# A depthwise 5x5 convolution moved from eight to sixteen tiles of the TensorE array, with its results kept by row phase

## The chip, the cores and the metric

The kernel runs on one core of a Trainium2 chip. The metric is the device time of one execution in microseconds. A core has a matrix engine (TensorE, PE in the profile; its weight loads are listed as PEld), a vector engine (VectorE, DVE), a scalar engine (ScalarE, ACT), GpSimd (POOL) and a queue that issues most DMAs (SyncE, SP). TensorE reads its operands from SBUF and writes to PSUM banks; the other engines copy results out of PSUM.

## The reference

The input x is (4, 128, 128, 128): four batches, 128 channels, 128 x 128 pixels, float32. The first layer is overlapping window attention and a gated feed-forward part with a depthwise convolution, the second a quantised pair of 3x3 convolutions:

```
# 9 x 9 overlapping regions of 16 x 16 pixels, step 14, 4 heads of 32
y = layernorm(tokens);  q, k, v = split(y @ w_qkv)
tok = softmax(q k^T / sqrt(32)) v @ w_out + b_out + tok
xf = overlap-average of tok            # (4, 128*128, 128)
y = layernorm(xf) @ w_p0 + b_p0        # 256 channels
ym = depthwise_conv5x5(y, dw_k, padding 2)
ym = batchnorm(ym over batch and pixels)
y = gelu(gelu(ym)) @ w_p2 + b_p2 + xf  # 128 channels
# second layer, x = y
q1 = round(15 clip(x, 0, 1)) ;  c1 = conv3x3(q1, quantised w1) ; batchnorm
q2 = round(15 clip(., 0, 1)) ;  c2 = conv3x3(q2, quantised w2) ; batchnorm
out = c2 + x
```

The batchnorm over all batches means that the gelu stage can start only when the depthwise convolution of all four batches is done, and likewise for the two later normalisations.

## The kernel before, in words

**Attention.** A band is one row of nine regions (j = 0 to 8); there are 36 bands, t = 0 to 35, nine for each batch. For region j of band t the order is written out by hand: `scores(j)` (L784; four heads side by side in four row tiles, into four PSUM banks held by two tiles `sc0` and `sc1`, one buffer each; ACT takes the exponentials, L792), then `values(j-1)` of the region before (L847, L855, into the bank `po`; DVE takes the reciprocal, L867, and two products), then four slots of side work that `beside(t)` plans: the layernorm and projections of band t+1 or t+2 (a1, a2), the output projection, second layernorm and 256-channel projection of band t-1 (b1, b2), and steps of the convolution (`c[j]`). `halves(j)` between the slots adds the two halves of the exponentials (POOL and DVE, L802). Every engine of the four named in MANUAL runs its instructions in this order; SP issues its DMAs in order too. `store` puts a DMA on a list, and `flush` issues after each step what was on the list before it.

**Layernorm by DMA.** The reciprocal deviations go to a row in DRAM (ACT's queue, L397) and come back spread over all partitions (`xn<-row`, L411, on SP).

**The depthwise convolution.** The projection's result y is stored to DRAM (`y_d<-y`, L431) as `y2_d`: rows, two column parities, 256 channels, 64 columns of one parity. Each channel is convolved as a banded matrix product: the contraction runs over 20 input rows x 2 parities (KD = 40 partitions), the output over 16 rows x 2 parities (32), and the columns are 8 row groups x 64 columns of a parity (512). Three shifts of one column make up the five columns of the kernel, accumulated in PSUM. Two halves of the partitions (row tiles of 64) and four column tiles hold eight channels at once: 24 matmuls for a tile of eight channels (`depthwise`, L601). A float32 matmul is two instructions in the profile. The result goes to two of the three `pm` banks, ACT copies both to SBUF (L648), DVE takes their statistics (L652), and they are stored to `cv_d` in rows of 64 floats (256 bytes). `conv_steps` gives 32 tiles for a whole batch (u loads for two tiles ahead, L634, weights, L587). Batches 0 to 2 are convolved beside the bands that start two after their last one: batches 0 and 1 over nine bands each (t = 10 to 27), batch 2 over five (28 to 32); of batch 3 four row groups over two bands, two over the last band, and the last two groups in `conv_rest` after attention, when the banks of the scores are free (L690, L721, L725, L730; weights by POOL's queue).

**Band matrices.** In the first ten bands a set of steps builds the banded weights in DRAM (`band_matrices`: `pad_d`, `band_d`, `dw_d`; 24 DVE copies at L268).

**Late stages.** `gelu_stage` reads `cv_d` in units of 8 rows (1024 pixels), applies batchnorm and two gelus on ACT (L1216, L1219), multiplies by w_p2 (L1228), adds xf on DVE (L1236; the convolution left each row as two parities, which this operation interleaves with a stride of two), stores the result to `id_d`, quantises it into `q1` (a padded fp8 image in SBUF), and runs the first 3x3 convolution (L1164, 18 matmuls a unit) two units behind. `last_stages` runs the second 3x3 convolution once for its statistics, three units behind the normalisation, keeps batch 3's result, and computes the others again in the last stage, where each unit is normalised, `id_d` is added and the output is stored (L1354).

## Time and profile before

| | us |
|---|---|
| median of 3 runs (lowest, highest) | 3247.21 (3236.61, 3251.82) |
| profiled execution | 3249.98 |
| its span | 3248.2 |

| stage of the profiled execution | from, to (us) |
|---|---|
| bands 0 to 9, no convolution | 27.1, 504.5 |
| bands 10 to 27, batches 0 and 1 convolved | 504.5, 1538.5 |
| bands 28 to 32, batch 2 convolved | 1538.5, 1911.9 |
| bands 33 to 35, batch 3 in part | 1911.9, 2193.6 |
| rest of batch 3's convolution | 2193.6, 2318.7 |
| gelu stage and first 3x3 convolution | 2318.7, 2798.2 |
| second 3x3 convolution | 2798.2, 3048 |
| last stage | 3048, 3248 |

A busy time is the time in which an engine had at least one instruction in flight; matmuls overlap, so a group's busy time divided by its count is far below the mean of one. The number behind the last bar of a group is the idle time just before its instructions, and what ended it. In the timeline, the first number is the start from the span's begin, the second the length of the merged stretch.

### The profile page before, as it was taken

Reading aid. Unit: us, or ns where it says so; the run is one execution under the profiler, and the core shown is the slowest. Engines: PE = TensorE matmul, PEld = TensorE weight load, DVE = VectorE, ACT = ScalarE, POOL = GpSimd, SP = SyncE. Lnnn points to the kernel's source line nnn. Section 1 sums busy time; section 2 is a strip of 40 time slices with the busy share of each in tenths; the row PEclk is TensorE's granted clock in tenths of the full one; section 3 lists DMA queues with packets and bytes.
Section 4 is the critical chain, followed back from the end, with each engine's and each line's share of the span. In section 5 each row is a group of like instructions: output and inputs, shape, how many; then the busy total and the mean of one; then the engine's idle time right before and its main releaser. Section 6 shows DMA issues by size and latency. Waiting matters only on the chain.

```text
span 3248.2 us, 92154 instructions
## 1 busy us (share of the span) xinstructions
PE 3059.6 (94%) x39162; PEld 1480.1 (46%) x39162; DVE 2014.5 (62%) x3244; ACT 1988.5 (61%) x2658; POOL 840.9 (26%) x1058
## 2 busy tenths in 40 slices
PE   7999999999999999999888998876899999999998
PEld 4555544444444444444344444453544444444443
DVE  5777886766766777676555664542455555666543
ACT  5777777777776777677555655432477777433443
POOL 3444443333333333333222232211111111000000
PEclk9999999999999999999999998876799999999999
DMA  3555677888886888886898988857899999452398
GB/s 82 151 167 162 176 186 191 203 199 204 215 193 169 191 206 211 196 213 172 179 202 201 209 188 203 196 158 187 264 354 359 358 359 304 162 167 80 110 357 311
DMA packets 809891, 681.70 MB, mean 210 GB/s; under 512 B 580918, under 2 KB 695935, under 8 KB 809471
## 3 DMA queue, kind: packets, MB, share of 16 engines
q1 hardware_dynamic: 798879, 669.17, 75.8%
q8 instruction: 311, 5.10, 0.7%
q0 software_dynamic: 1024, 3.93, 0.5%
q10 hardware_dynamic: 9568, 2.61, 0.3%
q14 instruction: 109, 0.89, 0.1%
HBM read 408.72 MB, written 270.79 MB: 209 GB/s over the span
## 4 chain that ended last, share of the span: by engine, by line
PE 76%; DMA 9%; ACT 5%; issue 4%; SPq 3%; DVE 2%; ACTq 0%; POOL 0%; DVEq 0%; POOLq 0%
PE pc L1164 21%; PE pm L438 16%; PE sc L784 9%; PE pm L601 9%; PE po L847 8%; PE pb L1228 6%; PE po L855 3%; DMA y_d<-y 3%; PE pm L377 3%; ACT pt L792 2%; DMA u<-y_d 2%; DMA xn<-row 1%; SPq L451 1%; SPq L431 1%; ACT v L775 1%
## 5 line engine op out<-in xcount | busy, mean ns | idle before, releaser
L867 DVE RECIPROCAL rd<-po 128x256 f32<-128x256 f32 x324 | 568.8, 1756 | 439.1 <-PE po L855 438.5
L1164 PE MATMUL pc<-q,wq 128*128 128x512 fp8e4 x3168 | 700.3, 381 | 5.1 <-DVE q L1176 5.1
L792 ACT ACTIVATE pt<-sc 128x1024 f32<-128x1024 f32 x648 | 628.2, 1025 | 119.1 <-PE sc L784 63.2
L802 POOL TENSOR_TENSOR sm<-pt 128x512 f32<-128x512 f32 x324 | 415.7, 1283 | 1047.3 <-ACT pt L792 727.0
L1164 PEld LDWEIGHTS <-wq 128*128 128x128 fp8e4 x3168 | 309.0, 98 | 406.7 <-issue 38.9
L784 PE MATMUL sc<-q,kr 32*128 32x256 f32 x5184 | 413.6, 417 | 27.3 <-ACT pt L792 27.1
L601 PE MATMUL pm<-u,w 40*32 40x504 f32 (+5 forms) x7680 | 369.6, 503 | 41.7 <-DMA u<-y_d 29.7
L784 PEld LDWEIGHTS sc<-q,kr 32*128 32x128 f32 x5184 | 254.1, 191 | 286.4 <-issue 177.1
L847 PE MATMUL po<-pt,v 128*32 128x256 f32 x5184 | 364.9, 401 | 10.0 <-DVE part L871 6.9
L648 ACT COPY c<-pm 128x512 f32<-128x512 f32 (+1 forms) x256 | 132.4, 563 | 272.3 <-PE pm L601 243.3
L438 PE MATMUL pm<-xn,wp 128*32 128x512 f32 (+1 forms) x2304 | 248.1, 553 | 44.6 <-ACT y L567 42.6
L567 ACT ACTIVATE y<-pm,vectors 128x512 f32<-128x512 f32 (+1 forms) x288 | 183.1, 641 | 166.0 <-DMA y_d<-y 111.9
L802 DVE TENSOR_TENSOR sm<-pt 128x512 f32<-128x512 f32 x324 | 244.2, 754 | 35.8 <-ACT pt L792 35.8
L438 PE MATMUL pm<-xn,wqkv 128*32 128x512 f32 (+1 forms) x2304 | 245.3, 548 | 4.9 <-ACT v L775 3.5
L601 PEld LDWEIGHTS pm<-u,w 40*32 40x32 f32 x7680 | 147.6, 112 | 223.1 <-issue 153.0
L652 DVE BATCH_NORM_STATS2 st<-c 128x6 f32<-128x512 f32 (+2 forms) x320 | 160.9, 550 | 134.8 <-ACT c L648 134.3
L1228 PE MATMUL pb<-cv,wp 128*128 128x512 f32 x512 | 232.1, 596 | 4.9 <-ACT cv L1219 4.9
L847 PEld LDWEIGHTS po<-pt,v 128*32 128x32 f32 x5184 | 140.5, 112 | 186.5 <-issue 103.5
L1172 DVE BATCH_NORM_STATS2 st<-pc 128x6 f32<-128x512 f32 x256 | 165.7, 689 | 84.7 <-PE pc L1164 84.7
L855 PE MATMUL po<-sm,ones 128*32 128x256 f32 x2592 | 206.1, 389 | 0.0
L874 POOL TENSOR_TENSOR ob<-ob,part 128x32 f32<-128x32 f32 x288 | 127.2, 442 | 230.6 <-DVE part L871 224.8
L438 PE MATMUL pm<-wqkv,yr 128*32 128x128 f32 x5184 | 176.3, 273 | 1.2 <-issue 1.2
(157 smaller groups left out, 3394.2 us busy)
## 6 DMA issues: line engine op xcount, KB each, us to landing
cv<-cv_d SPq DMA_DIRECT2D x64, 1024.0 KB
u<-y_d SPq DMA_DIRECT2D x234, 256.0 KB
cv_d<-c SPq DMA_DIRECT2D x192, 256.0 KB
y_d<-y SPq DMA_DIRECT2D x160, 256.0 KB
xn<-row SPq DMA_DIRECT2D x76, 512.0 KB
xfl<-xf_d SPq DMA_DIRECT2D x64, 512.0 KB
id_d<-y SPq DMA_DIRECT2D x64, 512.0 KB
idt<-id_d SPq DMA_DIRECT2D x64, 512.0 KB
```

The costliest lines, as they stand in the source:

```text
L438: nc.tensor.matmul(out[m], w[:, m], v, start=True, stop=True)
L567: nc.scalar.activation(y[:, :n], pm[:, : n * P].rearrange("p (r c e) -> p r e c", r=n, e=2), AF.Identity, bias=bp0[:, h : h + 1],)
L601: nc.tensor.matmul(outs[half][32 * q : 32 * q + 32, j, :, a:z], wt[hs, s, c, :], ut[hs, :, c, a + s - 1 : z + s - 1], start=(s == 1), stop ...
L784: nc.tensor.matmul(sc[h // 2][:, h % 2, kc, :].rearrange("p (r c) -> p r c", c=RS), region(kr, j)[hs, kc * P : (kc + 1) * P], queries(j, h ...
L792: nc.scalar.activation(pt, sc[p], AF.Exp)
L802: add(sm, pt[:, :, 0, :], pt[:, :, 1, :], ALU.add)
L847: nc.tensor.matmul(po[hs, 0, :], v[:, kc, hs], pt[h // 2][:, h % 2, kc, :], start=(kc == 0), stop=(kc == 1),)
L855: nc.tensor.matmul(po[hs, 1, :], ones, sm[h // 2][:, h % 2, :], start=True, stop=True)
L867: nc.vector.reciprocal(rd, po[:, 1, :])
L1164: nc.tensor.matmul(pc[:, h], w[:, t, :], q1[b][:, r + dy : r + dy + RB, dx : dx + P], start=(t == 0), stop=(t == 8),)
L1172: nc.vector.bn_stats(st[:, 2 * n + h, :], pc[:, h])
L1228: nc.tensor.matmul(pb[:, m], wp2[:, h, :], cv[:, h, px], start=(h == 0), stop=(h == 1))
```

## The change

The convolution is cut into sixteen tiles of 32 x 32. Output groups have 8 rows (GR = 8, sixteen groups), and the columns come in four phases (NC = 4), so that an output tile is 8 rows x 4 phases = 32; the contraction is 12 rows x 2 parities = 24 partitions (KD). Each of the four row tiles takes 64 of the 256 channels (channel 64 i + c is on partitions 32 i to 32 i + 23), the four column tiles take four channels; a step has sixteen channels. The input is still kept by two parities (IW = 64), so a matmul reads every second element; the five columns of the kernel and the four phases together need four shifts, so a step has 64 matmuls. The sixteen steps of a batch replace 32 tiles.

- A step writes to four banks, the two tiles of the score banks (`ps_s`), where a tile wrote to two of the three `pm` banks. ACT copies two banks out, DVE two (L687); statistics on DVE as before.
- Slots: even regions have the step first in the third slot, ahead of projections, odd ones last in the second. One or two steps a band take regions 4 and 8, then 2, 6, 0, and the odd ones last.
- Loads: a step of a whole batch reads two u tiles (three buffers in all) in sixteen DMAs and its weights in one. They are issued one step ahead, by a list `later` that runs after the next region's scores.
- `y2_d` is kept by row phase and parity, with channel and row group inside; a chunk of rows that crosses a group is stored in two DMAs. Input rows of a whole batch are read in runs of 4 KB. `cv_d` is kept so that a store writes 1 KB runs (half a batch) and a load of the gelu stage reads 4 KB.
- `conv_rest` has eight steps of 32 channels, which use the score banks and the `pm` and `po` banks in turn; its weights come in one DMA.
- The late stages go by row phase: a unit is 8 rows of one phase (every eighth row) of one half of the image, `xf_d` and `id_d` follow that order, the padded image `q1` holds phase by phase, the first 3x3 convolution runs three units behind and the second four. The second projection's sum on DVE now interleaves four phases (a stride of four elements), and an output unit is stored as eight rows of 512 bytes per channel.

```diff
-GR = 16
-CW = P // 2
+GR = 8
+NG = P // GR
+NC = 4
+CW = P // NC
+IW = P // 2
 KD = 2 * (GR + 4)
+NS = 16
...
-    y2_d = [dram.tile([P + 4, 2, 2 * P, CW], F32, name=f"y2_d{b}") for b in range(B)]
-    cv_d = [dram.tile([P // GR, 2 * P, GR * P], F32, name=f"cv_d{b}") for b in range(B)]
+    y2_d = [dram.tile([2 * GR, 2 * P, NG + 1, IW], F32, name=f"y2_d{b}") for b in range(B)]
+    cv_d = [dram.tile([2, 2 * P, 32, NG // 2, CW], F32, name=f"cv_d{b}") for b in range(B)]
...
+        def depthwise(outs, wt, ut):
+            for s, (a, z) in ((1, (0, CW)), (0, (1, CW)), (3, (0, CW - 1)), (2, (0, CW))):
+                for i in range(4):
+                    hs = slice(32 * i, 32 * i + KD)
+                    for q in range(4):
+                        nc.tensor.matmul(
+                            outs[i][32 * q : 32 * q + 32, :, a:z],
+                            wt[hs, s, q, :], ut(q)[hs, :, 2 * a + s - 1 : 2 * z + s - 2 : 2],
+                            start=(s == 1), stop=(s == 2),
+                        )
+        def fetch_input(ut, b, g, ch, below):
+            n, ng = ut.shape[1:3]
+            m = 8 if below else 2 * GR
+            for i in range(4):
+                at = 32 * i + 2 * GR * below
+                c = 64 * i + ch
+                nc.sync.dma_start(
+                    out=ut[at : at + m].rearrange("p c g x -> p c (g x)"),
+                    in_=y2_d[b][:m, c : c + n, g + below : g + below + ng].rearrange("p c g x -> p c (g x)"),
+                )
...
             def products(at):
-                k, jj, c0 = tiles[at]
-                ut, wt = U.pop(at), W[k, jj]
-                pc = [ps_m.tile([P, nj, ng, CW], F32, name="pm") for _ in range(2)]
-                depthwise(pc, wt[:, :, c0:], ut, nc_)
-                for half in range(2):
-                    cv = cp.tile([P, nj, ng, CW], F32, name=f"c{half}")
-                    nc.scalar.copy(
...
+                sc = [ps_s.tile([P, 2, 2, NT], F32, name=f"sc{p}") for p in range(2)]
+                banks = [
+                    sc[i // 2][:, i % 2].rearrange("p a n -> p (a n)")[:, : nk * w] for i in range(4)
+                ]
...
+                for i in range(4):
+                    cv = cp.tile([P, 2 * NT], F32, name="c")[:, : nk * w]
+                    (nc.vector.tensor_copy if i // 2 else nc.scalar.copy)(cv, banks[i])
+                    for m in range(nk):
+                        k = nk * at + m
+                        cm = cv[:, m * w : (m + 1) * w]
+                        nc.vector.bn_stats(stat(i, k, n), cm)
+                        gh = -(-ng // 8)
+                        store(results(b, g0, ng, i, k), cm.rearrange("p (h n) -> p h n", h=gh))
...
                 def one(at=at):
-                    if at + ahead < len(tiles):
-                        load(at + ahead)
+                    if at not in U:
+                        load(at)
                     products(at)
+                    if at + ahead < NS // nk:
+                        later.append(lambda: load(at + ahead) if at + ahead not in U else None)
...
-            for j in sorted((1, 3, 5, 7, 8, 4, 6, 2, 0)[: len(conv)]):
+            for j in sorted((4, 8, 2, 6, 0, 1, 5, 3, 7)[: len(conv)]):
...
-                ([a2[1]], [a1[4]], b1[:2], [*c[2], a2[2]]),
+                ([a2[1]], [a1[4]], [*c[2], *b1[:2]], [a2[2]]),
                 ([], [a2[3], *c[3]], [], [b1[2]]),
-                ([b1[3]], [a2[4]], [*a1[5:], *b2[:2]], [*c[4], b1[4]]),
+                ([b1[3]], [a2[4]], [*c[4], *a1[5:], *b2[:2]], [b1[4]]),
...
-                ([], [b2[6], x2], b1[7:], [*c[8], s1]),
+                ([], [b2[6], x2], [*c[8], *b1[7:]], [s1]),
...
                 for j, side in enumerate(beside(t)):
                     scores(j)
+                    while later:
+                        later.pop(0)()
...
-    units = [(b, k) for b in range(B) for k in range(NU2)]
+    units = [(b, h * GR + (k - 1) % GR) for b in range(B) for h in range(2) for k in range(GR)]
+    conv_units = [(b, k) for b in range(B) for k in range(2 * GR)]
...
+    def first_row(k):
+        return {-1: 0, GR - 1: 1, 0: NG + 1, GR: NG + 2}.get(k, NG + 2 + NG * k)
...
-                odd_even = lambda t: t.rearrange("p (n e) -> p n e", e=2)
-                pb_ = pb.rearrange("p m n -> p (m n)").rearrange("p (r e c) -> p r e c", e=2, c=P // 2)
+                by_phase = lambda t, e: t.rearrange("p (n e) -> p e n", e=NC)[:, 2 * e : 2 * e + 2]
                 for e in range(2):
                     nc.vector.scalar_tensor_tensor(
-                        odd_even(y)[:, :, e], pb_[:, :, e, :], bp2, odd_even(xf)[:, :, e], ALU.add, ALU.add
+                        by_phase(y, e), pb[:, e].rearrange("p (e n) -> p e n", e=2), bp2, by_phase(xf, e),
+                        ALU.add, ALU.add,
                     )
...
-                    out=out[b, :, 2 * RB * k : 2 * RB * (k + 1), :].rearrange("c r w -> c (r w)"), in_=z
+                    out=out[b, :, k // GR * 64 + k % GR : k // GR * 64 + 64 : GR, :],
+                    in_=z.rearrange("p (r w) -> p r w", w=P),
```

## The prediction

> **What bounds the kernel now.** I read the page's first two parts, then the busy time by stage, then the groups, then the order of time inside one band of attention. The stages: bands 0 to 9 without convolution, bands 10 to 27 (batches 0 and 1 convolved beside attention), bands 28 to 32 (batch 2), bands 33 to 35 (two thirds of batch 3), the rest of that convolution, the gelu stage, the second convolution, the last stage. The first lines give TensorE over the whole span, then the windows from the second stage to the last:
>
> ```profile
> PE 3059.6 (94%) x39162; PEld 1480.1 (46%) x39162; DVE 2014.5 (62%) x3244; ACT 1988.5 (61%) x2658; POOL 840.9 (26%) x1058
> ...
> PE   7999999999999999999888998876899999999998
> ```
> ```profile
> 504.50:1538.50 1034.00, 1012.27 (x16196) 478.96 (x16192) 723.21 (x1124) 742.41 (x1121) 376.67 (x478) 0.99 0.84 197
> 1538.50:1911.90 373.40, 341.31 (x5182) 155.85 (x5178) 217.60 (x338) 220.77 (x338) 104.40 (x133) 0.95 0.88 198
> 1911.90:2193.60 281.70, 234.17 (x4908) 135.84 (x4904) 134.90 (x273) 126.39 (x204) 56.47 (x69) 0.85 0.76 185
> 2193.60:2318.70 125.10, 83.12 (x2012) 56.79 (x2012) 44.00 (x180) 31.30 (x52) 13.94 (x27) 0.62 0.75 194
> 2318.70:2798.20 479.50, 472.49 (x1665) 209.68 (x1666) 262.26 (x398) 332.50 (x260) 72.12 (x78) 0.99 0.93 330
> 2798.20:3048.00 249.80, 249.80 (x1140) 111.44 (x1141) 166.96 (x261) 90.11 (x77) 0.00 (x0) 0.99 0.37 112
> 3048.00:3248.00 200.00, 190.38 (x878) 85.11 (x876) 79.64 (x71) 77.90 (x66) 0.55 (x1) 0.99 0.88 316
> ```
> Columns: window, length, busy time of PE, PEld, DVE, ACT, POOL, granted clock, DMA share, GB/s. In bands 10 to 27 TensorE is 98% busy; in the two windows after it DMA is at 0.88 and 0.76 while TensorE falls to 91% and 83%: waits set these. A band's own order shows what one convolution tile costs:
>
> ```profile
> 1184.81 0.61 PE L855 MATMUL po<-sm,ones 128*32 128x256 f32 x8
> 1185.35 2.78 PE L601 MATMUL pm<-u,w 40*32 40x512 f32 x48
> 1188.06 1.15 PE L784 MATMUL sc<-q,kr 32*128 32x256 f32 x16
> 1189.14 1.07 PE L847 MATMUL po<-pt,v 128*32 128x256 f32 x16
> ...
> 1190.89 3.62 PE L438 MATMUL pm<-xn,wp 128*32 128x512 f32 x32
> ```
> A tile of eight channels holds TensorE from 1185.35 to 1188.06: 2.71 us, and the next group follows with no gap. Bands 3 to 9 take 48 us, bands with four tiles 57: what a tile costs TensorE, it costs the band.
>
> ```profile
> L648 ACT COPY c<-pm 128x512 f32<-128x512 f32 x224 | 121.2, 590 | 215.7 <-PE pm L601 208.3 <-DMA u<-y_d 2.2 <-DVE xn L421 2.2
> L652 DVE BATCH_NORM_STATS2 st<-c 128x6 f32<-128x512 f32 x192 | 123.7, 684 | 50.3 <-ACT c L648 50.0
> L1236 DVE SCALAR_TENSOR_TENSOR y<-pb,vectors,xfl 128x512 f32<-128x512 f32 x128 | 90.2, 746 | 138.7 <-PE pb L1228 129.3 <-DMA xfl<-xf_d 8.6 <-DMA id_d<-y 0.8
> L792 ACT ACTIVATE pt<-sc 128x1024 f32<-128x1024 f32 x648 | 628.2, 1025 | 119.1 <-PE sc L784 63.2 <-ACT rstd L392 48.6 <-PE po L855 3.6
> ```
> The copies and statistics of a tile (0.59 and 0.68 us) and the two exponentials that empty the score banks (1.03 us each) are the prices for the part below.
>
> **The change, part by part.**
>
> *The matmuls.* A tile of eight channels is 24 matmuls, two instructions each, on eight array tiles: six waves. In the trace the first instructions of successive waves start at 1001.407, 1001.830 and 1002.252 us: 423 ns a wave at 504 columns. All eight tiles run at once. The new step of sixteen channels is 64 matmuls, 128 instructions on sixteen tiles: eight waves. At 512 columns a wave should be 427 ns (the unpacked 512-column matmul of the gelu stage takes 3.43 us per 8 instructions, 429 ns). So 8 x 427 = 3.42, plus 0.15 for the change of array mode as now (2.71 - 6 x 0.427), is 3.57 us per step, against 2 x 2.71 = 5.42. A batch: 16 x 3.57 = 57.1 against 32 x 2.71 = 86.7. Instructions of a wave start 7 ns apart, 16 x 7 = 112 ns, well inside the wave. The moving operand is now read with a stride of two floats; no TensorE row of before does that. Bounds: nothing (DVE's stride-two second projection takes 746 ns, its contiguous twin of the same size, at L549, 741), or double, 854 ns a wave, if the gaps are streamed too. I take nothing, the row that is strided, and keep double for the range.
>
> The Trainium skill (TensorE: Matmul & The Clock Gate, Part 3: Packing small matmuls — row/col tiling) speaks against me: sixteen tiles measured 10.6 times one, not 16. By that a wave is 427 x 16/10.6 = 645 ns, a step 5.3 us, and 48 full steps would cost 84 us more than in my sum. Its figure is for one burst; the trace's eight tiles repeat without loss, so I keep the row. The same skill (SBUF — State Buffer, Door 1: The DMA port swizzle) asks for two accesses per 16-byte line for full rate: the strided stream has just two, the second projection, now at stride four, one.
>
> *Bands 10 to 27* (1034 us). Less 64 x 2.71 = 173.4, plus 32 x 3.57 = 114.2. New: the step sits in the score banks, so it waits for the exponentials of its own region, and the next scores wait for its copies. With two steps a band these stand in regions 4 and 8. After a step DVE does statistic, statistic (each behind an ACT copy), copy, statistic, copy: 0.8 + 2 x 0.68 + 0.65 + 0.68 + 0.65, 4.2 us until the last bank is free. Region 4 has 5 us of projections behind the step (3.5 + 1.4): nothing lost. Region 8 has 3.6: 0.6 lost, and 0.4 before the step, where 1.8 us of other work face 2.1 us of exponentials. 16 x 1.0 = 16. Sum -43. Two copies of 0.59 a step leave ACT and two come to DVE (70% busy here): on neither path.
>
> *Batch 2* (373.4 us). By groups 320 is TensorE's work (five bands of 46.7 and 86.7), 53 waits. After: 290; hand-overs 15, since regions 2 and 6 have less work behind the step (1.9 and 3.0 us against 4.2). A step's loads are 17 issues on SP (16 of u, one of w; 0.39 us each in bands 21 to 24), issued in the next region, queued behind the step's four stores, which wait for the DVE copies: 4.2 + 1.5 + 6.6, and some 3 us to land, 15 us, where the next step comes after 11 to 13. Three in four steps lose 3 us: 12 steps, 36 us. Behind these issues stand xn loads and y stores: xn is needed a region later, where DVE has slack. Against this DMA gets lighter: by the packet records (256 B 19 ns, 1 KB 80, 4 KB 212 when loaded) a batch's results go from 65,536 x 19/16 = 78 us of the sixteen engines to 16,384 x 80/16 = 82 at most, 47 at the unloaded 46 ns; the inputs, half as many shared rows more, from 102 to 81. I leave a third of the old waits, 18. 290 + 15 + 36 + 18 = 359: -14.
>
> *Bands 33 to 35* (281.7 us). TensorE's work 211, waits 71. The convolution falls from 71 to about 47 (waves of half and a quarter length, 213 and 107 ns, as now). Steps stand in nearly every region; the odd ones have nothing behind them: about 2.6 us (copies of 0.37) and 0.8 before, four a band, 41 us, 3 in the even ones. Half of the old waits lie under these. 140 + 47 + 44 + 36 = 267: -15.
>
> *Rest of batch 3.* From 2257 to 2307 us, 50 us at a clock near 0.6. Sixteen tiles take half the waves; DVE then sets it: per step two copies 0.74, eight statistics 1.65, eight merges 1.53, eight steps 31 us, some 36 with the start. Loads of 1 KB rows instead of 4 KB give 4 back. -10.
>
> *Late stages.* A convolution now needs one unit more ahead of it: about 1.5 us at the start of each of two stages, +3. The gelu stage has 7.34 us of TensorE per unit (3.43 + 3.91); DVE is busy 262 of 479.5 there, and were its stride-four operation to double (+95) it would still be covered. Output rows leave as 512-byte packets, eight where one of 4 KB went: 8 x 27 = 216 ns against 159 (unloaded) or 180 (loaded). A unit's load and store need 1.27 + 1.73 = 3.00 us at least, 64 units 192 us, with loaded values 203, where TensorE needs 188. Bounds +4 and +25; +10. xf leaves in 512-byte packets too, 0.5 us of DMA a chunk, under attention. Band preparation loses 16 of 24 DVE copies of 1.2 us in bands where TensorE sets the pace: 0. More y stores (288 to 368): SP has room, a band's issues now take 32 of 57 us.
>
> **Sum**, against the profiled execution's 3250.0: -43 - 14 - 15 - 10 + 3 + 10 = -69, 3181; it lies 3 above the median, so 3178, said as 3180.
>
> **Rivals.**
> - *Sixteen tiles or the stride lengthen the wave* (ends slower). One mechanism, in the step's matmuls. For: no row shows 4 x 4 tiles or a strided stream. Against: the eight-tile waves, and four row tiles of the scores that write four banks at full pace. Break-even: 48 full steps and about 16 in shorter waves share 69 us, about 1.2 us a step, a wave of 580 ns instead of 427. At 854 ns: 32 x 3.4 + 16 x 3.4, less what lies under waits, about +140: 3320. Chance 0.15.
> - *The banks cost more than the array gives back.* For: DVE is 70% busy, its copies stand behind reciprocals of 1.76 us; ACT may still be in the exponentials. If every full step lost the whole 4.2 us, 48 x 4.2 = 202, of which 67 is in my sum: 3315; half of that excess, 3245. Against: regions 4 and 8 hold most of the steps of two batches, with 3.6 to 5 us of cover. Chance 0.17, mostly 3215 to 3290.
> - *SP and DMA hold bands 28 to 35 where they were*: no gain there, 3210; with the last stage at +25, 3225. Chance 0.08.
> - *The old waits of those bands go with the small packets*: 18 + 36 less, and no late loads: 3090 to 3120. Chance 0.08.
>
> **The numbers.** My case 0.52, from 3120 to 3225. Under half a per cent (16 us) this kernel's runs tell nothing. Faster: 0.52 + 0.08 + 0.06 of the third and a little of the second: 0.68. Within 0.5%: 0.08. Slower: 0.24. The range takes in the fourth rival's lower part and the slower ones to 3300.
>
> **What would show it.** The matmuls of a step: 128 instructions in 3.4 to 3.6 us, waves of 427 ns. Bands 10 to 27 near 990 us. Waits of scores on the copies under 1 us at region 8 and none at region 4; waits of the convolution on u loads only from band 28 on. Last stage 200 to 215 us. Wrong if waves run past 580 ns, if DVE's copies stand behind its reciprocals in most steps, or if the last stage is held by DMA well beyond 215 us.

## The result, and the profile after

The changed kernel takes 4209.96 us in the median of four runs (4199.62 to 4217.23), the kernel before 3241.91. The ratio is 1.298, with a 95% interval of 1.293 to 1.303: 30% slower, where 3180 us was forecast and 3300 was the upper end of the range. The profiled execution took 4199.62 us, its span is 4197.8.

The page's first two parts for the changed kernel (busy time; the span in 40 slices, and the granted clock in tenths):

```profile
PE 3322.5 (79%) x42234; PEld 1632.9 (39%) x42234; DVE 2139.1 (51%) x3388; ACT 1937.7 (46%) x2546; POOL 831.1 (20%) x1043
...
PE   8998887766777777677677777677765999999999
...
PEclk9999998887888888888877777778765999999999
```

TensorE was 94% busy and is now 79%. A slice is 105 us; the convolution runs from the sixth slice to the thirty-first. From the seventh on TensorE's digits are 7 and less and the granted clock is at 8 and less, and both come back when the convolution ends. The same eight stages as in the table of before, from the windows of the changed kernel (length; busy time of PE, PEld, DVE, ACT, POOL; clock; DMA share; GB/s):

```profile
28.40:538.30 509.90, 464.06 (x7084) 242.23 (x7080) 365.65 (x564) 356.91 (x528) 212.83 (x262) 0.98 0.58 153
538.30:2113.00 1574.70, 1116.23 (x17220) 570.80 (x17216) 762.20 (x1187) 720.84 (x1056) 374.78 (x477) 0.84 0.58 135
2113.00:2706.40 593.40, 435.69 (x5694) 205.14 (x5690) 239.15 (x372) 206.36 (x308) 103.62 (x133) 0.74 0.64 134
2706.40:3075.30 368.90, 271.04 (x5861) 148.20 (x5859) 152.65 (x319) 116.06 (x190) 56.29 (x69) 0.77 0.79 149
3075.30:3248.40 173.10, 89.43 (x2590) 54.47 (x2588) 51.79 (x198) 26.43 (x50) 8.21 (x17) 0.60 0.74 150
3248.40:3745.70 497.30, 484.21 (x1665) 205.49 (x1666) 313.42 (x398) 332.50 (x259) 70.67 (x74) 0.99 0.90 318
3745.70:4000.10 254.40, 253.49 (x1152) 112.43 (x1153) 167.29 (x261) 91.11 (x78) 0.00 (x0) 0.98 0.33 110
4000.10:4197.80 197.70, 187.64 (x865) 83.72 (x863) 79.52 (x70) 77.04 (x65) 0.55 (x1) 0.98 0.98 320
```

Of some 950 us more, 541 lie in bands 10 to 27 and 220 in bands 28 to 32. No engine is busy for more than 71% of the second window, and DMA for 58% of it, less than the 84% of before: nothing is at its limit, so something waits. The list of waits of the changed kernel for that window, DVE's and then PE's (engine, line, what it waited for: us in total, times, longest), followed by the same two lines of the kernel before for its own bands 10 to 27:

```profile
DVE xn L431 <- DMA xn<-row: 429.7, 32, 15.7
...
PE po L879 <- DVE part L903: 412.3, 54, 14.3
```
```profile
DVE xn L421 <- DMA xn<-row: 13.5, 10, 2.7
...
PE po L847 <- DVE part L871: 0.4, 1, 0.4
```

DVE waits for the layernorm's rows 32 times, as often as there are steps of the convolution, and PE waits for DVE by nearly the same sum. The timeline of the changed kernel around one step shows how they hang together (start, length, engine, line, operation, count; in brackets the idle time before it and what ended it):

```profile
1003.81 4.72 PE L613 MATMUL sc<-u,w 24*32 24x512 f32 x128
...
1015.15 16.21 SPq L628 DMA_DIRECT2D u<-y_d  x16
...
1031.40 0.85 SPq L421 DMA_DIRECT2D xn<-row  x2
...
1037.62 1.29 DVE L431 TENSOR_TENSOR xn<-xn,xf 128x512 f32<-128x512 f32 x2 [14.17 <-DMA xn<-row]
1038.83 1.75 DVE L899 RECIPROCAL rd<-po 128x256 f32<-128x256 f32 x1
...
1041.25 1.94 PE L879 MATMUL po<-pt,v 128*32 128x256 f32 x16 [11.88 <-DVE part L903]
```

After the step SP issues the sixteen u loads of the next one. They hold it for 16.2 us, a microsecond each. The xn load stands behind them; it is issued at 1031.40 and its rows are there at 1037.62, when DVE has been waiting for 14 us. DVE works in order, so the reciprocal of a region stands behind that wait, and the values of the next region behind the reciprocal. When TensorE goes on its first instructions run slowly: these sixteen took 1.94 us, and 1.07 in the regions without a wait. So not all of the loss is idle time: by the windows TensorE is busy for 1116 us of these bands at a granted clock of 0.84, and for 1050 us at 0.98 with the same instructions in run e4 below, where no loads stand in the way. In the kernel before the same place of the queue looks like this:

```profile
1185.98 0.36 SPq L411 DMA_DIRECT2D xn<-row  x1
...
1187.05 1.51 SPq L634 DMA_DIRECT2D u<-y_d  x4
```

Why a microsecond each? SP's entries in the trace show that every DMA signals one of eight semaphores, taken in turn by SP's and ACT's DMAs alike, and that an issue waits for the one that it will signal itself. So eight are under way, and an issue waits for the DMA eight places ahead of it. Here six loads went out by 1017.70. The seventh waited for the weights; the eighth went out at 1019.50, when the first had landed (one of the eight places was that of ACT's `row<-rstd`), and the next four a microsecond apart, as the loads ahead of them landed. The thirteenth went out at 1030.06: its semaphore had last been given to ACT's `row<-rstd`, issued at 1025.65 and landed 4.4 us later. And the loads land slowly: the first four, 128 KB each, a microsecond apart, and between 1015 and 1032 us the middle 4 KB packet took 460 ns, where the quickest tenth took 159. SP's list of waits for bands 10 to 27 has the two terms:

```profile
SPq L628 <- DMA row<-rstd: 218.0, 48, 7.1
SPq L628 <- DMA u<-y_d: 106.5, 105, 4.3
```

The loads of these 32 steps hold SP for 554 us, 17.2 a step. Some 10 us of that are waits between issues: 6.8 for ACT's row and 3.3 for u loads that have to land first. The issues themselves take the rest, under 7 us.

### The profile page after: what moved, and what is told of

It reads as the page before. It is cut to its first block, busy times and chain, and to the rows that moved or that the text cites. A ratio compares the mean times of both kernels' runs of the same rounds, so it can differ in the third digit from the quotient of the medians.

```text
span 4197.8 us, 98725 instructions
## 1 busy us (share of the span) xinstructions
PE 3322.5 (79%) x42234; PEld 1632.9 (39%) x42234; DVE 2139.1 (51%) x3388; ACT 1937.7 (46%) x2546; POOL 831.1 (20%) x1043
## 5 line engine op out<-in xcount | busy, mean ns | idle before, releaser
L879 PE MATMUL po<-pt,v 128*32 128x256 f32 x5184 | 402.2, 434 | 478.1 <-DVE part L903 477.9
L816 PE MATMUL sc<-q,kr 32*128 32x256 f32 x5184 | 492.7, 423 | 109.0 <-ACT pt L824 59.7
L613 PE MATMUL sc<-u,w 24*32 24x496 f32 (+5 forms) x10240 | 420.0, 606 | 147.9 <-DMA u<-y_d 120.0
L816 PEld LDWEIGHTS sc<-q,kr 32*128 32x128 f32 x5184 | 289.4, 192 | 384.2 <-ACT pt L824 159.2
L613 PEld LDWEIGHTS sc<-u,w 24*32 24x32 f32 x10240 | 220.2, 114 | 301.2 <-issue 179.7
L687 ACT COPY c<-sc 128x512 f32<-128x512 f32 (+1 forms) x144 | 67.6, 517 | 534.8 <-PE sc L613 440.2
L431 DVE TENSOR_TENSOR xn<-xn,xf 128x384 f32<-128x384 f32 (+1 forms) x140 | 83.7, 638 | 389.3 <-DMA xn<-row 389.3
L807 ACT COPY v<-pm 128x512 f32<-128x512 f32 (+1 forms) x180 | 97.9, 544 | 378.4 <-PE pm L448 377.7
L448 PE MATMUL pm<-xn,wqkv 128*32 128x512 f32 (+1 forms) x2304 | 261.7, 575 | 10.8 <-ACT v L807 3.7
L431 DVE TENSOR_TENSOR xn<-xn,xt 128x384 f32<-128x384 f32 (+1 forms) x140 | 82.8, 633 | 310.5 <-DMA xn<-row 310.5
```

Source lines behind the costliest of these rows:

```text
L431: nc.vector.tensor_tensor(t, by, src()[:, hh * n // 2 : (hh + 1) * n // 2], ALU.mult)
L448: nc.tensor.matmul(out[m], w[:, m], v, start=True, stop=True)
L613: nc.tensor.matmul(outs[i][32 * q : 32 * q + 32, :, a:z], wt[hs, s, q, :], ut(q)[hs, :, 2 * a + s - 1 : 2 * z + s - 2 : 2], start=(s == 1) ...
L816: nc.tensor.matmul(sc[h // 2][:, h % 2, kc, :].rearrange("p (r c) -> p r c", c=RS), region(kr, j)[hs, kc * P : (kc + 1) * P], queries(j, h ...
L879: nc.tensor.matmul(po[hs, 0, :], v[:, kc, hs], pt[h // 2][:, h % 2, kc, :], start=(kc == 0), stop=(kc == 1),)
```

## The experiments

Stage lengths in us by each run's profile, and its time. Each run was made once, beside one of the kernel before on the same chip, which took 3231 to 3245 us; differences under half a per cent (16 us) say nothing.

| run | 0-9 | 10-27 | 28-32 | 33-35 | rest | gelu | time |
|---|---|---|---|---|---|---|---|
| before | 477 | 1034 | 373 | 281 | 126 | 479 | 3242 |
| changed | 510 | 1575 | 593 | 368 | 174 | 497 | 4210 |
| e1 other order of loads | 514 | 1506 | 548 | 327 | 173 | 497 | 4047 |
| e2 spread over regions | 514 | 1444 | 632 | 368 | 174 | 495 | 4108 |
| e3 both | 516 | 1396 | 576 | 330 | 167 | 495 | 3962 |
| e4 no u loads | 513 | 1144 | 365 | 368 | 178 | 495 | 3545 |
| e5 no u loads, no stride | 516 | 1140 | 368 | 368 | 177 | 495 | 3544 |
| e6 sum not interleaved | 517 | 1578 | 595 | 371 | 170 | 481 | 4192 |
| e7 a quarter of the bytes | 514 | 1223 | 393 | 372 | 177 | 495 | 3657 |
| e8 all bytes in four wide loads | 514 | 1168 | 410 | 372 | 177 | 498 | 3618 |
| e9 loads on POOL's queue | 509 | 1215 | 413 | 376 | 174 | 496 | 3665 |
| e10 no u loads, projections moved | 518 | 1214 | 386 | 372 | 172 | 495 | 3640 |
| e11 no u loads, batch 3 too | 513 | 1145 | 375 | 298 | 172 | 495 | 3480 |
| e12 before, loads cut in two | 474 | 1183 | 421 | 324 | 129 | 479 | 3490 |
| e13 as e9, other order of matmuls | 512 | 1219 | 422 | 381 | 172 | 496 | 3681 |
| e14 before, stores cut | 491 | 1034 | 372 | 286 | 124 | 480 | 3266 |
| e15 as e9, batch 3 too | 512 | 1237 | 415 | 357 | 172 | 495 | 3667 |

### e1, e2, e3: the order and the place of the loads

```diff
-        def fetch_input(ut, b, g, ch, below):
+        def fetch_input(ut, b, g, ch, below, tiles=range(4)):
...
-            for i in range(4):
+            for i in tiles:
...
-                    for below in range(2):
-                        fetch_input(ut, b, g0, 4 * k + nc_ * m, below)
+                    for i in (0, 2, 1, 3):
+                        for below in range(2):
+                            fetch_input(ut, b, g0, 4 * k + nc_ * m, below, (i,))
```


> Only the order of the sixteen u loads of a step is changed: row tile 0, then 2, then 1, then 3, each with its 16-partition and its 8-partition load, instead of all four 16-partition loads and then all four 8-partition ones. Theory Q (the sixteen loads hold SP's queue for 17 us a step, and the xn loads of the layernorm behind them come late): the time falls only if the hold does. Theory P (the hold itself is so long because neighbouring loads write to the same few partitions, a 4 KB packet taking 460 ns in the middle where it took 159 at best): the hold falls from 17 to about 10 us, 4 KB packets to about 250 ns in the middle, and with some 7 us less at each of about 45 steps the time falls to 3850 to 3950. If the hold is only a matter of the number of loads in flight at a fixed latency: 17 us stays, 4150 to 4220. Rival B (the hand-over of the score banks) and rival W (longer waves of the matmuls): no change, 4200.

4047 us: 163 less. The hold of a step in bands 10 to 27 fell from 17.2 to 15.6 us in the middle, and the 4 KB packets there from 334 ns in the mean to 284. The direction is that of theory P, the size is not: it expected 7 us off a hold, which lost 1.6, and 260 to 360 us off the whole.

```diff
-                    while later:
-                        later.pop(0)()
+                    for p, n in list(later):
+                        for _ in range(n):
+                            if p:
+                                p.pop(0)()
...
```
(The rest of the edit puts a step's loads on the list `p` instead of issuing them; n is six, or nine for batch 2.)

> The weights and the sixteen u loads of a step, in their old order, are issued in parts: six after the scores of each following region for batches 0 and 1 (nine for batch 2), instead of all seventeen after the scores of the next one. Theory Q: no xn load stands behind more than six or nine u loads; the wait of DVE for xn falls from 700 us to under 150, bands 10 to 27 from 1575 to 1030 to 1150 us, the whole to 3400 to 3600 (batch 2 keeps part of its loss, since its steps are two regions apart). Rivals B and W: the work and its order on PE, ACT and DVE is the same, so 4100 to 4200.

4108 us: theory Q failed by its number. DVE's wait for xn fell from 700 to 471 us over the whole span (430 to 258 in bands 10 to 27), not under 150, since SP is still held for 467 us by the loads of bands 10 to 27 (554 in the changed kernel), and each part stands ahead of some xn load. Batch 2, with steps two regions apart, got worse.

> Both edits together. Theory Q with P: 3250 to 3450, 100 us or more under the spread alone, most of it in bands 28 to 35. Q without P: the same as the spread alone within 30 us. Rivals B and W: 4100 to 4200.

3962 us, in none of the three ranges. The gains of the two edits nearly add (163 and 102 alone, 248 together), but 720 us over the kernel before remain: neither the order nor the place of these sixteen loads on this queue is what matters most.

### e4: no loads

```diff
+                if ng == NG and at:
+                    U[at] = U[0]
+                    return
...
-                us, ws = U.pop(at), W.pop(at)
+                us, ws = U[at], W.pop(at)
```


> Left out: the u loads of fifteen of the sixteen steps of batches 0 to 2; every step is convolved from the first one's data. All else, the weight loads and the results' stores too, is as it was. This shows what the rest of the change costs. Theory Q: bands 10 to 27 at 1034 - 173 + 32 x 4.65 (a step as the trace now shows it where TensorE is warm) + 16 = 1025, 1000 to 1060 us, batch 2 290 to 360; with batch 3 and the later stages as they are now (87 + 48 + 20 over before) and 32 in bands 0 to 9: 3350 to 3430. Rival B: the steps still cost some 20 us each over the sum, over 3900. Rival W: as B, with waves as long as in the changed kernel and no waits between.

3545 us, 665 less, and above the 3350 to 3430 of theory Q. The loads of batches 0 to 2 are most of the loss, but not all of it: bands 10 to 27 take 1144 us, not 1000 to 1060. The waits of e4 in bands 10 to 27, DVE's and then PE's, and one of its steps in the timeline:

```profile
DVE xn L431 <- DMA xn<-row: 24.0, 2, 12.1
...
PE po L882 <- DVE part L906: 46.7, 38, 9.8
PE sc L819 <- ACT pt L827: 37.4, 70, 1.7
```
```profile
1270.90 4.67 PE L613 MATMUL sc<-u,w 24*32 24x512 f32 x128
```

The wait for xn is gone with the loads. What is left: a step takes 4.60 us in the middle, and PE waits 84 us for exponentials and DVE's products, 11 before. No scores wait for a copy of the step here (the list has none): rival B's hand-over is not it. The waits lie in the regions that held a tile of 2.7 us and now hold nothing: some 2.5 us of TensorE work, while two exponentials of 1.0 us each have to be waited for.

### e5, e13: why a step takes 4.6 us

```diff
-                            wt[hs, s, q, :], ut(q)[hs, :, 2 * a + s - 1 : 2 * z + s - 2 : 2],
+                            wt[hs, s, q, :], ut(q)[hs, :, a : z],
```


> The kernel without u loads once more, and the matmuls of the convolution read each row's first columns in a row instead of every second one (left out beside the loads: the parity and the shift of the columns, so the convolution's values are not the kernel's). A step there takes 4.65 us where the prediction had 3.57. If the stride is what lengthens the waves: 3.6 to 3.8 us a step, some 1 us less at each of 64 steps, 3470 to 3500. If the sixteen pairs of weight load and matmul of a wave are (the trace shows them 16.5 ns apart in every second wave, where eight tiles followed at 7): 4.6 to 4.7 us again, 3530 to 3560.

3544 us, and 4.34 us a step instead of 4.60. The stride of two costs 0.26 us of the 1.03 that a step has over the forecast. The larger part stays. In e4's trace the first wave's instructions start 7 ns apart, as with eight tiles, but those of the third, for example, 16.5 ns apart, each behind its own weight load, which takes 260 ns for sixteen before the next wave can follow.

```diff
-                for i in range(4):
...
-                    for q in range(4):
+                for q in range(4):
+                    for i in range(4):
...
```
(on top of e9's edit, below)

> The changed kernel with the u loads on POOL's queue, and the sixteen matmuls of a shift in another order: the four row tiles inside, the column tiles outside. If the order in which the tiles of the array are loaded makes a wave longer (four neighbours share their rows now): a step falls from 4.6 to under 4.2 us, or rises over 5. If the number of instruction pairs does: 4.5 to 4.7 and 3650 to 3680, as with the old order.

A step takes 4.93 us in the middle, 4.76 in e9, on which it is built (3681 us in all, no difference that counts). That lies between the two ranges of the expectation. The order matters a little, and the old one is the better. Of the two explanations the number of pairs is left, but it is argued and not shown: no run had fewer pairs.

### e7, e8: number, bytes or width of the loads

```diff
                 if ng == NG and at:
                     U[at] = U[0]
+                    for m in range(nu):
+                        for below in range(2):
+                            fetch_input(U[0][m][:, :, :4], b, 0, 4 * k + 2 * m, below)
                     return
```
(on top of e4's edit)

> The kernel without u loads, with the sixteen loads of a step put back at a quarter of their bytes: the same number of DMAs, queues and places in the order, rows of 1 KB instead of 4 KB (left out: three quarters of the input, so fifteen of sixteen steps mix two steps' data). If the number of DMAs holds SP (sixteen issues, eight in flight, a fixed latency): a hold of 13 to 17 us and 3950 to 4200. If the bytes do, on the few partitions that they go to: a hold of 6 to 8 us (sixteen issues at 0.4) and 3560 to 3700.

3657 us, 112 over e4, with a hold of 7.4 us a step: sixteen issues of a quarter of the bytes are cheap. SP now waits hardly at all between them (15.3 us for ACT's row and 11.1 for u loads in bands 10 to 27).

```diff
+                    flat = y2_d[b].rearrange("m c g x -> (m c g x)")
+                    for m in range(nu):
+                        for h in range(2):
+                            n = 768
+                            nc.sync.dma_start(
+                                out=U[0][m].rearrange("p c g x -> p (c g x)")[:, h * n : h * n + n],
+                                in_=flat[(2 * m + h) * P * n : (2 * m + h + 1) * P * n].rearrange("(p n) -> p n", n=n),
+                            )
...
```
(on top of e4's edit, after `U[at] = U[0]`)

> The kernel without u loads, with all of a step's bytes put back in four DMAs over all 128 partitions in rows of 3 KB instead of sixteen over 16 or 8 partitions each (left out: which data they are; the values are not the kernel's). If bytes as such are too many at this place: 3900 to 4200, as the changed kernel. If the narrow loads are the cause, few partitions each and sixteen of them: 1.57 MB at the last stage's 320 GB/s are 5 us of DMA, hidden: 3550 to 3650.

3618 us, 73 over e4. One group of these loads in e8's timeline:

```profile
1002.91 2.98 SPq L670 DMA_DIRECT2D u<-y_d  x4
```

All of the 1.57 MB of a step go in four issues that hold SP for 2.1 us in the middle, and the 3 KB packets take 121 ns in the middle. So neither the bytes alone (73 us) nor the sixteen issues alone (112) make the 665. What is left is the two together: many loads, each of full size, on a queue that lets eight be under way, so that SP waits for what was issued eight places earlier. How much of it is the number of the full-size loads and how much the few partitions of each is not shown: e8 changed both, and no run had sixteen loads of full size over all partitions.

The Trainium skill (SBUF — State Buffer, Door 1: The DMA port swizzle) has the rule: DMA bandwidth follows the number of SBUF ports that the partitions reach; partitions 0 to 15 reach four of sixteen ports and measured 104 GB/s with transfers of 1 MiB, and a range 32 higher reaches the same ports. Row tiles 0 and 1 share their ports so, and 2 and 3 theirs. An estimate from that page, with half of its rate for two ports and one pair after the other: two loads of 128 KB on four ports take 2.5 us, four such loads 5, the four of 64 KB as long again, and the two u tiles of a step 20. SP is held 17.2, but 6.8 of that are waits for ACT's row, so that the nearness of the two numbers proves nothing. The runs agree in kind (e1, which alternates the pairs, is shorter, if only by 1.6 us a step, and e8, over all partitions, is fast). The prediction cited this very section, for another sentence of it.

### e9, e15: another queue

```diff
-                nc.sync.dma_start(
+                (nc.gpsimd if g == 0 and ng == NG else nc.sync).dma_start(
```


> The changed kernel with the u loads of batches 0 to 2 issued on POOL's queue instead of SP's; the same loads, bytes and partitions. If the harm is done by SP's queue alone (xn loads standing behind sixteen issues): DVE's wait for xn in bands 10 to 27 falls from 387 us to under 100, and as far as POOL itself is not held the time falls towards 3600; POOL is held for sixteen issues a step, though, and the sums of halves and with them the values wait for it. If POOL is held as SP was, the wait moves there: values wait for POOL's sums, 3900 to 4300. If the loads' traffic alone delays the xn loads (same DMA engines, wherever they are issued), the wait for xn stays above 250 us.

3665 us, with the same loads, bytes and partitions. The waits of e9 in bands 10 to 27, DVE's and PE's:

```profile
DVE xn L431 <- DMA xn<-row: 13.1, 12, 3.5
...
PE sc L816 <- ACT pt L824: 39.7, 67, 3.2
PE po L879 <- DVE part L903: 27.7, 37, 0.9
```

DVE's wait for xn is back at the 13 us of the kernel before. POOL issues eight of the loads in a row (4.2 us) and the others one by one between its sums, and it has the time. 545 us of the loss are gone by an edit of one line: the loads did their harm from SP's queue, by standing ahead of the xn loads. What of that queue it was this run doesn't tell apart: on POOL's the loads also leave the DMA queue that SP feeds and the turn of eight semaphores that they shared with ACT's row (POOL's entries have eight of their own), and they go out over a longer time. e9 still takes 120 us more than e4, 71 of them in bands 10 to 27; they are not traced to one cause.

> The changed kernel with all u loads beside attention on POOL's queue, batch 3's too. If SP's queue is what bands 33 to 35 lose: 376 us there with batch 3 on SP falls to 300 to 330, 3600 to 3630 in all. If the transfers themselves are late wherever they are issued: 360 to 380, 3650 to 3680.

3667 us: bands 33 to 35 fell from 376 to 357 us and the whole did not. The 357 lie between the two ranges, nearer to the second: most of what that stage loses stays when its loads leave SP's queue. The whole decides nothing, since bands 10 to 27, in which the two kernels do the same, took 22 us longer here. What the loads of bands 33 to 35 cost in all, e11 shows below.

### e12: the same harm done to the kernel before

```diff
-                    for a, z in ((0, GR), (GR, GR + 4)):
+                    for a, z in ((0, 8), (8, GR), (GR, GR + 2), (GR + 2, GR + 4)):
```


> The kernel before, with each of its u loads cut in two: 16 and 4 partitions each instead of 32 and 8, eight DMAs a tile instead of four, the same bytes in the same rows. Sixteen channels then take sixteen narrow loads as in the changed kernel, but in two groups of eight at different places of the order. If narrow loads hold SP by their number and their few partitions wherever they stand: 1.6 us a group grows to 4 to 8 us and the time to 3300 to 3600. If it needs sixteen in a row: 3240 to 3270.

3490 us, 257 more, with nothing changed but the width and the number of the u loads. Two groups of loads in its timeline, and its wait for xn in bands 10 to 27:

```profile
1308.99 5.55 SPq L634 DMA_DIRECT2D u<-y_d  x8
...
1320.06 6.74 SPq L634 DMA_DIRECT2D u<-y_d  x7
```
```profile
DVE xn L421 <- DMA xn<-row: 109.5, 31, 6.7
```

Eight loads of 16 and 4 partitions hold SP for 6.3 us in the middle, where four of 32 and 8 partitions held it for 1.6, and the wait for xn grows from 13.5 to 109.5 us. Sixteen in a row are not needed. The way from SP to TensorE is another one here, though. TensorE's longest wait in these bands, in e12 and then in the kernel before:

```profile
PE pm L438 <- ACT y L567: 81.5, 12, 7.6
```
```profile
PE pm L438 <- ACT y L567: 7.0, 6, 2.7
```

ACT's y waits in turn for the stores of y (154.6 us, 31.2 before), which stand behind the loads on SP as the xn loads do. And what SP itself waits for at these loads is above all ACT's row (110.9 us) and the xn loads (52.7), and the u loads for 15.9 only. So the number of the loads, which fills the turn of eight, may matter more here than their width; the run changed both.

### e6, e10, e11, e14: the smaller terms

```diff
-                        by_phase(y, e), pb[:, e].rearrange("p (e n) -> p e n", e=2), bp2, by_phase(xf, e),
+                        y[:, U // 2 * e : U // 2 * (e + 1)], pb[:, e], bp2, xf[:, U // 2 * e : U // 2 * (e + 1)],
```


> The changed kernel with the second projection's sum on DVE written and read in rows of 512 floats without interleaving the phases (left out: the order of the pixels, so the image is not the kernel's). If the stride of four (1.16 us an operation against 0.75 before) pushes the statistics, the copy on ACT and with it the gelus behind PE's turn: the gelu stage falls from 497 to 479 to 483 us, the rest stays, 4180 to 4200. If something else makes a unit 7.55 us (the third unit of lag, DMA): 495 to 499.

The gelu stage takes 481 us, as the first theory has it. The group in the changed kernel, and then in e6 (mean ns of one behind the busy time):

```profile
L1282 DVE SCALAR_TENSOR_TENSOR y<-pb,vectors,xfl 128x512 f32<-128x512 f32 x128 | 141.9, 1159 | 104.6 <-PE pb L1275 103.0 <-DMA id_d<-y 1.5
```
```profile
L1282 DVE SCALAR_TENSOR_TENSOR y<-pb,vectors,xfl 128x512 f32<-128x512 f32 x128 | 90.3, 747 | 139.5 <-PE pb L1275 130.9 <-DMA xfl<-xf_d 6.4 <-DMA id_d<-y 2.2
```

A stride of four makes the operation 1159 ns, half as long again. The statistics behind it on DVE come later, ACT's copy waits for those, the next gelus stand behind the copy, and TensorE's weight loads wait for the gelus in nearly every unit (63 times, 38.3 us; 5 times and 7.7 us in the kernel before).

```diff
-                ([b1[3]], [a2[4]], [*c[4], *a1[5:], *b2[:2]], [b1[4]]),
-                ([], [b1[5], *c[5]], [], [b2[2]]),
+                ([b1[3]], [a2[4]], [*c[4], *b2[:2]], [b1[4]]),
+                ([], [b1[5], *c[5]], [*a1[5:]], [b2[2]]),
...
-                ([], [b2[5], x1, *c[7]], [], []),
-                ([], [b2[6], x2], [*c[8], *b1[7:]], [s1]),
+                ([], [b2[5], x1, *c[7]], [*b1[7:]], []),
+                ([], [b2[6], x2], [*c[8]], [s1]),
```
(on top of e4's edit)

> The kernel without u loads, with two groups of projections moved out of the regions that hold a step: those of the next band from region 4 to region 5, the last ones from region 8 to region 7. In that kernel no scores wait for a copy of the step, but the regions without work (2.5 and 3.1 us) wait for exponentials (37 us) and for DVE's products (47 us) in bands 10 to 27, and a band takes 62 us where it took 57 before. If the bare regions are the cause of what is left: 58 to 60 us a band, 3490 to 3520. If the hand-over of the banks then shows instead (less work behind the step): scores wait for copies, 1 to 2 us a step, 3530 to 3600.

3640 us, 95 more than e4. The waits for exponentials and products fell to less than half (17 and 16 us), but the hand-over came in their place. PE's waits in e10, bands 10 to 27:

```profile
PE sc L819 <- DVE c L690: 60.1, 31, 2.1
...
PE sc L819 <- ACT c L690: 13.2, 15, 0.9
```

So the projections behind a step do cover the copies, as the prediction had it for region 4, and whoever takes them away pays 2.3 us a step (73 / 32). The two waits are the ends of one choice. They are not all of the 71 us by which bands 10 to 27 grew: TensorE's busy time rose too, from 1050 to 1078 us, at a granted clock of 0.94 instead of 0.98.

```diff
-                if ng == NG and at:
+                if at:
                     U[at] = U[0]
```
(against e4's edit)

> As the kernel without u loads, but the loads of batch 3's steps beside attention are left out too (after each unit's first). If its narrow loads are what makes bands 33 to 35 87 us longer than before: 368 falls to 270 to 300 us there, 3450 to 3480 in all. If the hand-over of the banks at every region does: 340 to 368, 3515 to 3545.

Bands 33 to 35 fall to 298 us: 70 of their 87 are loads too.

```diff
-                        store(
-                            xf_d[b][:, (i * STEP + r) * P : (i * STEP + r + n) * P],
...
+                        cut = min(n, 8 - row % 8)
+                        for a, z in ((0, cut), (cut, n)):
+                            if z > a:
+                                store(xf_d[b][:, (row + a) * P : (row + z) * P], held["xf"][:, a * P : z * P])
```
(and the stores of y likewise)

> The kernel before, with its stores of xf and y cut where a chunk of rows crosses a group of eight, as the changed kernel cuts them; the same bytes. If the extra issues on SP delay the layernorm's loads: bands 0 to 9 take 490 to 510 us instead of 477, and the whole grows by 20 to 60. If the new matrices' transfers in bands 6 to 9 do instead: 475 to 480 and 3230 to 3260 in all.

Bands 0 to 9 grow by 14 us to 491, the other stages hardly. That is less than half of the 32 that the changed kernel loses there, at the lower edge of what the first theory had. The rest is not traced to a cause.

## Why the prediction was wrong

*The step that failed: the u loads.* The prediction priced "17 issues on SP" at 0.39 us each, 6.6 us a step, from rows in which four stood together, and for batch 2 alone. In bands 10 to 27, where 32 of the 48 full steps lie, it gave them no price at all. Of what stands behind them it said "xn is needed a region later, where DVE has slack". Measured: a hold of 17.2 us, not 6.6; DVE's waits for the rows, up to 15.7 us long; and by the loads in all 431 us in bands 10 to 27 and 228 in batch 2 (changed kernel less e4), 659 of the 1019 by which the profiled span missed the forecast (4197.8 against 3179). The issues themselves took under 7 us a step, about what it had said. What it put at nothing are the waits between them, some 10 us. Two errors lie in it. The price was taken from a row with four loads in flight, and the new step has sixteen, with eight allowed in a turn that ACT's row shares. And DMA was counted in bytes and packet sizes: loads of 32 partitions became twice as many of 16, which no row of before shows, and e12 shows what that change of number and width does to the kernel before. The 4 KB packets, priced at no more than 212 ns, took 334 in the mean there. In batch 2 the prediction did have steps that wait for their loads, at 36 us; TensorE's list has 93.8 us for u loads there, and 45.5 for DVE's products behind the rows.

*The matmuls.* Forecast 3.57 us a step and "16 x 7 = 112 ns, well inside the wave"; measured 4.60 in e4. The waves are (4.60 - 0.15) / 8 = 556 ns in the mean, not 427. That is at most 66 us over 64 steps (if batch 3's shorter ones lose as much), nearly all of the gain of 69 in its sum: the first rival, with its break-even of 580 ns, was almost right in size and by itself would have ended near no change. The eight tiles' rows could not show it. The figure of the Trainium skill (TensorE: Matmul & The Clock Gate, Part 3: Packing small matmuls — row/col tiling), 10.6 for sixteen tiles, by which a wave would be an estimated 645 ns, was nearer than the row that the prediction kept, though the cause here is in part the stride (0.26 us a step). Of the prediction's sentence on accesses per line the runs bear out the half on the stride of four (1159 ns against 747 in e6); a stride of two costs DVE nothing, but TensorE those 0.26 us (e5).

*The score banks.* Forecast 16 us in bands 10 to 27. No scores wait for copies there in e4, so the cover was at least what it took it for, and e10 shows what that cover was worth. What it lacked is the other side: the regions that lose their tiles are left with less work than their exponentials take. 84 us of waits instead of 11.

*Bands 33 to 35*, forecast -15: +87, of it 70 loads (e11). *Rest of batch 3*, forecast -10: +48. No run was made for it; the profile has TensorE waiting for the first loads there and a clock of 0.60, as before. *Bands 0 to 9*, forecast 0 with "SP has room": +32, of which cut stores explain 14.

*Late stages.* Forecast +13. The last stage is unchanged (197.7 us, and 197.4 before when both are cut at the first matmul of the third convolution pass), so the 512-byte rows cost nothing. The gelu stage lost 18, because "were its stride-four operation to double (+95) it would still be covered" looked at DVE's busy time and not at who stands behind the operation.

*The third rival* named SP and DMA, but for bands 28 to 35 alone, and as a gain withheld and not as a loss. Even with nearly all u loads beside attention left out the change would have lost 7% (e11, 3480). e9, the fastest version that computes what the kernel has to, takes 3665, 13% over the kernel before: nothing here beats that one.

## What to carry to other kernels

When loads are regrouped, price them by what stands behind them in their queue: count how many go out together, how many may be in flight, whose transfers they then wait for, and how many partitions each one reaches, and not bytes and packet sizes alone. A queue that also carries a latency-bound load (here the layernorm's rows) should not carry the bulk; another engine's queue with time to spare took back 545 us by an edit of one line. And when work is moved out of a region, look at what it covered there, not only at what covers it in its new place.

## What the runs showed of the hardware that was not expected

- Sixteen loads of 128 or 64 KB to 16 or 8 partitions each held SP's queue for 17.2 us a step, the same bytes in four loads over 128 partitions for 2.1. Number and width were not changed apart.
- SP's and ACT's DMAs took eight semaphores in turn, so that an issue on one queue waited for a transfer of the other: 218 us of the 554 for which the u loads held SP in bands 10 to 27.
- Sixteen 32x32 tiles with a weight load for each instruction do not run back to back: 4.60 us for eight waves that would stream in 3.42 at the 427 ns of an eight-tile wave; a moving operand of every second float costs 0.26 us of it.
- The second projection's sum on DVE costs nothing for a stride of two (746 ns, and 747 without a stride in e6), and takes 1159 ns with a stride of four.
